# Turns by TensorE transposes, k and v without padding columns, a head start for the second image's front, and x1 added in PSUM in the last image

## The chip, the cores and the metric

The kernel runs on one core of a Trainium2 chip, in one launch. The metric is device time in microseconds (us). Three runs of the kernel before took 5461.75, 5472.33 and 5480.27 us; their median is 5472.33 us. All data are float32.

## What is computed

The input x is a batch of 8 images of 256 channels and 64 x 64 pixels. Two residual layers follow each other; `_gn` is a group norm over groups of 8 channels, without weights:

```python
# layer 0: local attention with 4 heads over 3 x 3 neighbours, and generated kernels
qkv = einsum('oc,bchw->bohw', w_qkv, gn(x))          # q, k, v of 256 channels each
attn = softmax(sum_d(q * k_patch), over 9 neighbours)
kernel = einsum(w_kg, qkv by head) + b_kg            # 4 heads x 9 weights at each pixel
x1 = x + w_proj @ (alpha * sum(kernel * v_patch) + beta * sum(attn * v_patch))
# layer 1: modulated deformable 3 x 3 convolution
om = conv3x3(gn(x1), w_off) + b_off                  # 27 = 18 offsets + 9 mask values
v = bilinear_samples(gn(x1), 9 taps, offsets) * sigmoid(mask)
out = x1 + einsum('bckhw,ock->bohw', v, w)
```

## The kernel before, in words

An image is cut into 8 chunks of 8 rows (512 pixels); 256 channels lie as 2 tiles of 128 partitions. There are two streams of work.

The **front** of an image is a Python generator (`fronts`) that issues 144 steps. The first 126 are `attention`. After four steps of group norm (means, an empty one, the standard deviation with `ready`, the first `normed`), each chunk takes 14 steps: the spread weights of the chunk before, q, k(0), k(1), products(0), products(1), logits, generated, v(0), turned, v(1), project, weights, keys. The work on a chunk's output is finished during the steps of the next chunk. The last 18 steps are `prepare`: per chunk, one step turns the 27 offset values of the chunk before to pixel-major (`positions`) and writes normed pixels to a table in DRAM (`to_table`), and one step runs the 3 x 3 offset convolution (`offsets`).

The **slots** of an image are 72, one for each chunk and tap (8 x 9). A slot gathers 4 blocks of 128 rows from the table by indirect DMA (`gather`, L820, on POOL), scales the first corner (`scale`, L836, on ACT), adds the three other corners (`sum_corners`, L844, on DVE), transposes the sums on TensorE (`transposes`, L865, with copies by ACT at L868), and multiplies them with the convolution weights into the PSUM tile `po` (`product`, L890). After 9 taps `finished` copies `po` to `y` (ACT, L901) and `stored` adds x1 (DVE, L906) and sends the chunk out (SP).

The order on every engine is the order of the Python program (`manual_schedule`); each engine runs its own instructions strictly in that order, and waits are semaphores between engines. The main loop at the end of the kernel runs over 577 slots in two halves each. In each half it issues the slot's work, and then as many front steps of the next image as the `goal` (L963) asks for: one for each half slot, and 12 more spread over the first image (`STEPS_AHEAD`). So the whole front of image 0 runs alone, then 7 images of slots run with the front of the next image between them, and the slots of the last image run alone. The gathers run 18 blocks ahead of the transposes.

Places that matter for what follows:

- `keyed` (L329 to 343), called by `k` and `v`: a step computes 4 rows for both channel tiles, 264 columns for each matmul since the 2 padding columns of each row are computed too, and ACT copies PSUM to `kt` (L349) or, in overlapping 10-column tiles, to `vt` (L358).
- `generated` and `turned` (L405 to 439): the 36 generated kernel values come out of TensorE in two halves of 64 partitions, one for each channel tile; ACT copies them (L417). Four float32 matmuls with `gs` as weights and the constant `stk_gen` as moving operand turn them and add the two halves in one (L427); DVE adds the bias (L435).
- `offsets` and `positions` (L695 to 775): the same for the 27 offset values, which come out in four groups of 32 partitions; four matmuls with `stk_om` turn and add them (L718), ACT makes the mask (L732), DVE computes positions from PSUM (L735) and then indices and weights (L736 to L768). DVE's L735 waits for ACT's L732, since both read one PSUM tile.
- A chunk's `r` is a tile for x1 of images 0 to 6, loaded from DRAM by SP (L877).
- `psum_a` hands out four PSUM buffers in turn, for nearly all front work.

Of the kernel before, what the change touches and what calls it, by code (L numbers as in the profile page):

```python
# [9 lines left out]
F32 = mybir.dt.float32  # L10
I32 = mybir.dt.int32
AF = mybir.ActivationFunctionType
# [5 lines left out]
P = 128  # L18
C = 256
# [32 lines left out]
LEAD = SCALE_AHEAD + GATHERS  # L52
STEPS = 2 * SLOTS
STEPS_AHEAD = 12


@with_exitstack
def preact_kernel(ctx: ExitStack, tc: tile.TileContext, a: dict, out: bass.AP):
# [34 lines left out]
    def const_tile(name, shape, queue=nc.scalar):  # L93
        t = const.tile(shape, F32, tag=name, name=name)
        queue.dma_start(t, a[name])
        return t
# [12 lines left out]
        load_chunk(0, c, nc.scalar)  # L109
    alpha = const_tile("alpha", [P, 1])  # L110
    gmat = const_tile("gmat", [P, P])
    bkg = const_tile("bkg", [P, HEADS * KK])
    w_qkvT = const_tile("w_qkvT", [P, NT, 3 * C])
    ident = const_tile("ident", [P, P])
    near_k = const_tile("near_k", [P, NK])
# [8 lines left out]
    stk_om = const_tile("stk_om", [P, NOM], nc.sync)  # L124
    stk_gen = const_tile("stk_gen", [P, HEADS * KK], nc.sync)
# [15 lines left out]

    kt = const.tile([P, NT, R + 2, WP], F32, tag="k", name="k")
    vt = const.tile([P, NT, TC, KT, KT], F32, tag="v", name="v")

    w_effT = const.tile([P, NT, P // 2], F32, tag="w_effT", name="w_effT")
    nc.vector.memset(w_effT, 0.0)
# [25 lines left out]
    def psum_a(name):  # L172
        return ps_a.tile([P, 512], F32, tag="a", name=name)
# [86 lines left out]
            )  # L260
        return xn

    def tiled(ps, rows):

        t = ps[:, : rows * WP].rearrange("p (r w) -> p r w", w=WP)
        t = t[:, :, 0 : TC * T].rearrange("p r (t x) -> p t r x", x=T)
        ap = [list(d) for d in t.ap]
        ap[-1][1] = KT
        return bass.AP(tensor=t.tensor, offset=t.offset, ap=ap)

    def window(t, ct, k):
        dy, dx = divmod(k, 3)
# [17 lines left out]
    class Attention:  # L290
# [35 lines left out]
                    vt[:, :, :, R : R + 2, :].rearrange("p c t y x -> p (c t) (y x)"),  # L326
                )

        def keyed(self, which, i, to):  # L329

            for lo, hi in [(0, 2)] * (self.c == 0 and i == 0) + [(2 + 4 * i, 6 + 4 * i)]:
                for m in range(NT):
                    ps = psum_a(f"ps{'qkv'[which]}_{self.u}_{lo}_{m}")
                    o = which * C + m * P
                    for ct in range(NT):
                        nc.tensor.matmul(  # L336
                            ps[:, : (hi - lo) * WP],
                            w_qkvT[:, ct, o : o + P],
                            self.xn[:, ct, lo:hi, :],
                            start=(ct == 0),  # L340
                            stop=(ct == NT - 1),
                        )
                    to(m, lo, hi, ps)

        def k(self, i):
            self.keyed(
                1,
                i,
                lambda m, lo, hi, ps: nc.scalar.copy(  # L349
                    kt[:, m, lo:hi, :].rearrange("p r w -> p (r w)"), ps[:, : (hi - lo) * WP]  # L350
                ),
            )

        def v(self, i):
            self.keyed(
                2,
                i,
                lambda m, lo, hi, ps: nc.scalar.copy(vt[:, m, :, lo:hi, :], tiled(ps, hi - lo)),  # L358
            )

        def products(self, jj):

# [42 lines left out]
        def generated(self):  # L405

            ps = psum_a(f"gen_{self.u}")
            for ct in range(NT):
                nc.tensor.matmul(
                    ps[64 * ct : 64 * ct + 64, :],  # L410
                    w_effT[:, ct],
                    window(self.xn, ct, 4),
                    start=True,
                    stop=True,
                )
            self.gs = gs = p1.tile([P, N], F32, tag="gs", name=f"gs_{self.u}")
            nc.scalar.copy(  # L417
                gs.rearrange("p (t y x) -> p y t x", y=T, x=T),
                ps.rearrange("p (y t x) -> p y t x", y=T, x=T),
            )  # L420

        def turned(self):

            ps = psum_a(f"gt_{self.u}")
            n = HEADS * KK
            for j in range(NB):
                nc.tensor.matmul(  # L427
                    ps[:, j * n : (j + 1) * n],
                    self.gs[:, j * P : (j + 1) * P],
                    stk_gen,  # L430
                    start=True,
                    stop=True,
                )
            self.kb = kb = p1.tile([P, self.G, KK], F32, tag="kb", name=f"kb_{self.u}")
            nc.vector.tensor_add(  # L435
                kb.rearrange("p (j h) k -> p j (h k)", j=NB),
                ps[:, : NB * n].rearrange("p (j k) -> p j k", j=NB),
                bkg.unsqueeze(1).to_broadcast([P, NB, n]),
            )

        def softmax_1(self):
# [228 lines left out]
    def prepare(b, gn):  # L670
# [43 lines left out]
        def positions(c, om):  # L714
            u = f"{b}_{c}"
            ps = psum_a(f"omt_{u}")
            for j in range(NB):
                nc.tensor.matmul(  # L718
                    ps[:, j * NOM : (j + 1) * NOM],
                    om[:, j * P : (j + 1) * P],  # L720
                    stk_om,
                    start=True,
                    stop=True,
                )
            omt = ps[:, : NB * NOM].rearrange("p (b o) -> p b o", o=NOM)
            S = [P, NB, 2 * KK]

            def small(name, shape=S, dt=F32):
                return p1.tile(shape, dt, tag=name, name=f"{name}_{u}")

            mk = small("mk", [P, NB, KK])
            nc.scalar.activation(mk, omt[:, :, 18:27], AF.Sigmoid)  # L732

# [137 lines left out]
    def product(b, n, m):  # L871

        c, k = divmod(n, KK)
        if k == KK // 2 and m == 0:
            r = p1.tile([P, NT, N], F32, tag="r", name=f"r_{b}_{c}")
            if b + 1 < B:
                nc.sync.dma_start(r, kept[b % 2][:, :, c * N : (c + 1) * N])  # L877
            state["r"] = r
        if k == 0 and m == 0:

            if b + 1 == B and c % 2:
                state["po"] = [psum_a(f"po_{b}_{c}_{i}") for i in range(NT)]
            else:
                po = ps_o.tile([P, NT, 512], F32, tag="o", name=f"po_{b}_{c}")
                state["po"] = [po[:, i, :] for i in range(NT)]
        po, v = state["po"], state["v", n]
        if m == NT - 1:
            del state["v", n]
        for ct in range(NT):
            nc.tensor.matmul(  # L890
                po[m],
                w_conv[:, ct, k, m * P : (m + 1) * P],
                v[:, ct, :],
                start=(k == 0 and ct == 0),
                stop=(k == KK - 1 and ct == NT - 1),
            )

    def finished(b, c, m):
        if m == 0:
# [17 lines left out]
    with tc.manual_schedule(engines=ordered):  # L917
# [2 lines left out]
            first_stats(0, c)  # L920
        fold(ps)
        steps = fronts()
        done = 0
        while done < STEPS:
            next(steps, None)
            done += 1
# [12 lines left out]
        gather(SUM_AHEAD + GATHERS + 1)  # L939
        last = None  # L940
        for n in range(B * SLOTS + 1):
# [3 lines left out]
            for m in range(NT):  # L945
# [14 lines left out]
                        stored(*last, slice(m, m + 1))  # L960

                h = NT * n + m + 1
                goal = h * STEPS + min(h, STEPS) * STEPS_AHEAD  # L963
                while (done - STEPS) * STEPS < goal:
                    next(steps, None)
                    done += 1


def _constants():
# [17 lines left out]
    stk_om = np.zeros((P, NOM), f)  # L987
    for g in range(4):
        stk_om[32 * g : 32 * g + NOM] = np.eye(NOM, dtype=f)
    base = np.zeros((P, NC * NB, KK, 2), f)  # L990
    base[..., 0] = (2 * np.arange(NC * NB)[None, :, None] + p[:, None, None] // W) + k // 3 - 1
    base[..., 1] = (p[:, None, None] % W) + k % 3 - 1
# [4 lines left out]
        "near_k": np.concatenate([near.T, near.T]),  # L997
        "turn_y": turn_y,
        "turn_x": turn_x,
        "stk_om": stk_om,  # L1000
        "stk_gen": np.tile(np.eye(P // 2, HEADS * KK, dtype=f), (2, 1)),
        "base": base.reshape(P, NC * NB, 2 * KK),
        "ident": np.eye(P, dtype=f),
    }
# [2 lines left out]
def _laid_out(x, w_qkv, w_kg, b_kg, alpha, beta, w_proj, w_off, b_off, w):  # L1007
# [2 lines left out]
    off[..., :NOM] = w_off.reshape(NOM, NT, P, KK).transpose(2, 1, 3, 0)  # L1010
    boff = np.zeros((P, 1), np.float32)
    boff[:NOM, 0] = b_off
    return {
        "x": x.reshape(x.shape[0], C, L),
        "w_qkvT": w_qkv.reshape(3 * C, NT, P).transpose(2, 1, 0),
        "w_qkv": w_qkv.reshape(8, 96, C).transpose(1, 0, 2),
        "w_kgT": w_kg.reshape(HEADS, KK, 2, 96).transpose(3, 0, 2, 1).reshape(96, 8, KK),
        "bkg": np.broadcast_to(b_kg.reshape(1, HEADS * KK), (P, HEADS * KK)),
        "alpha": np.broadcast_to(alpha.reshape(1, 1), (P, 1)),
        "beta": np.broadcast_to(beta.reshape(1, 1), (P, 1)),  # L1020
        "w_projT": w_proj.reshape(C, NT, P).transpose(2, 1, 0),
# [24 lines left out]
```

## Time and profile before

One profiled execution took 5417.27 us, with a span of 5415.5 us from its first to its last instruction. It is shorter than the median of the plain runs by 55.06 us (1.0%).

| what | number |
|---|---|
| median of three runs | 5472.33 us |
| profiled execution, its span | 5417.27 us, 5415.5 us |
| mean granted TensorE clock | 0.942 |
| gather DMA issues on POOL (L820) | 2304, 1291 ns mean |
| corner sums on DVE (L844) | 6912, 2811.7 us busy |
| convolution matmuls (L890) | 4608 instructions, 2255.0 us busy |
| k and v matmuls (L336) | 2176 instructions, 254.5 and 259.5 us busy |
| turn of the generated kernels (L427) | 512 instructions, 69.3 us busy |
| turn of the offsets (L718) | 512 instructions, 63.1 us busy |
| adds of x1 in the last image (L906) | 7 of 1214 ns, 2 of 693 ns |

In the profile, PE is TensorE's matmuls, PEld its weight loads, DVE the VectorE, ACT the ScalarE, POOL the GpSimd (which issues the gathers), and SP the queue of the plain DMAs. A float32 matmul that is not a transpose shows as two instructions, each with a weight load (2304 calls at L890 give 4608 instructions); a transpose shows as one. The mean duration of a matmul [...] overlaps with the next one, so for throughput the busy time of a group, or the distance from one start to the next, is read.

### The profile page before, as it was taken

The numbers are of one execution on the slowest core, as the hardware profiler recorded it, in microseconds if no ns is written. First come the engines' busy times: TensorE is split into PE (matmuls) and PEld (weight loads), VectorE is DVE, ScalarE is ACT, GpSimd is POOL, SyncE is SP. The second block draws the span as 40 slices with busy tenths as digits, with TensorE's granted clock in tenths as the row PEclk, the third lists the DMA queues.
The fourth block names the chain that finished last, engine by engine and source line by source line (L and its number), as shares of the span: only waits on it lengthen the run. The fifth ranks groups of instructions, "written<-read, shape, count | busy, mean of one in ns | idle before, by whom it ended". The sixth has DMA issues, their size and how long they took to land. (4 is left out here: it accounts for less than half of the span.)

```text
span 5415.5 us, 80013 instructions
## 1 busy us (share of the span) xinstructions
PE 4849.9 (90%) x26848; PEld 2762.1 (51%) x26848; DVE 4185.3 (77%) x10066; ACT 2447.4 (45%) x5312; POOL 2976.4 (55%) x2310
## 2 busy tenths in 40 slices
PE   8989999999898999999999998989999899987777
PEld 5545554555545555555555555455554555543333
DVE  5577878787787877878788787877878787777666
ACT  3344444444444444444444444444444444444343
POOL 0045554655555556455555555565654655656776
PEclk9999999999999999999999999999999999998888
DMA  2177779777697778877788777877779777688877
GB/s 91 55 253 259 253 244 330 245 249 271 242 330 270 254 264 286 307 249 262 251 310 286 265 256 256 313 266 263 260 244 332 249 248 265 235 288 307 306 268 264
DMA packets 472650, 1414.24 MB, mean 261 GB/s; under 512 B 46815, under 2 KB 114655, under 8 KB 472109
## 3 DMA queue, kind: packets, MB, share of 16 engines
q0 software_dynamic: 331776, 1208.11, 63.4%
q1 hardware_dynamic: 138444, 197.65, 10.3%
q8 instruction: 211, 3.46, 0.2%
q10 hardware_dynamic: 2016, 3.38, 0.2%
q14 instruction: 203, 1.65, 0.1%
HBM read 1276.02 MB, written 132.94 MB: 260 GB/s over the span
## 5 line engine op out<-in xcount | busy, mean ns | idle before, releaser
L820 POOL DMA_INDIRECT g<-table,idx x2304 | 2973.9, 1291 | 2418.0 <-DVE s L844 808.9
L844 DVE SCALAR_TENSOR_TENSOR s<-g,wt,s 128x256 f32<-128x256 f32 x6912 | 2811.7, 476 | 307.6 <-ACT s L836 240.7
L890 PE MATMUL po<-vt,w_conv 128*128 128x512 f32 x4608 | 2255.0, 616 | 33.9 <-ACT y L901 22.4
L836 ACT ACTIVATE s<-g,wt 128x256 f32<-128x256 f32 x2304 | 1068.2, 510 | 574.8 <-DMA g<-table,idx 471.4
L890 PEld LDWEIGHTS po<-vt,w_conv 128*128 128x128 f32 x4608 | 842.0, 198 | 816.8 <-issue 760.1
L868 ACT COPY vt<-pt 128x512 f32<-128x512 f32 x1152 | 618.2, 588 | 528.9 <-PE pt L865 352.5
L865 PE MATMUL pt<-ident,s 128*128 128x128 f32 x4608 | 698.1, 294 | 170.1 <-ACT vt L868 125.6
L865 PEld LDWEIGHTS pt<-ident,s 128*128 128x128 f32 x4608 | 569.3, 151 | 402.6 <-ACT vt L868 166.3
L383 DVE TENSOR_TENSOR qk<-qk,near_k 128x400 f32<-128x400 f32 x256 | 135.4, 567 | 545.8 <-remote 445.7
L375 PE MATMUL qk<-k,q 64*64 64x100 f32 x4096 | 207.4, 268 | 166.5 <-issue 162.1
L304 PE MATMUL psq<-xn,w_qkvT 128*128 128x512 f32 x512 | 258.4, 650 | 65.0 <-DVE wk L516 63.5
L556 ACT COPY acc<-av 128x512 f32<-128x512 f32 x128 | 75.1, 587 | 483.3 <-PE av L549 337.4
L702 PE MATMUL om<-xn,w_off 128*32 128x512 f32 x2304 | 288.6, 596 | 0.6 <-DVE pos L735 0.5
L375 PEld LDWEIGHTS qk<-k,q 64*64 64x64 f32 x4096 | 137.0, 139 | 291.3 <-issue 253.5
L336 PE MATMUL psv<-xn,w_qkvT 128*128 128x264 f32 (+1 forms) x1088 | 259.5, 383 | 0.0
L336 PE MATMUL psk<-xn,w_qkvT 128*128 128x264 f32 (+1 forms) x1088 | 254.5, 379 | 0.0
L336 PEld LDWEIGHTS psv<-xn,w_qkvT 128*128 128x128 f32 x1088 | 201.5, 191 | 85.3 <-issue 49.5
L336 PEld LDWEIGHTS psk<-xn,w_qkvT 128*128 128x128 f32 x1088 | 201.7, 190 | 82.6 <-issue 38.8
L561 PE MATMUL proj<-acc,w_projT 128*128 128x512 f32 x512 | 240.8, 593 | 0.7 <-ACT acc L556 0.7
L549 PEld LDWEIGHTS av<-wk,vk 100*64 100x64 f32 x4096 | 166.0, 163 | 97.9 <-issue 39.9
L549 PE MATMUL av<-wk,vk 100*64 100x64 f32 x4096 | 190.3, 253 | 26.9 <-issue 21.6
L312 ACT COPY q<-psq 128x512 f32<-128x512 f32 x128 | 74.0, 584 | 310.6 <-PE psq L304 310.6
(94 smaller groups left out, 3397.8 us busy)
## 6 DMA issues: line engine op xcount, KB each, us to landing
table<-ts SPq DMA_DIRECT2D x384, 176.0 KB
g<-table,idx POOLq DMA_INDIRECT x2304
out_dram<-r SPq DMA_DIRECT2D x63, 512.0 KB
x<-in_x_dram SPq DMA_DIRECT2D x61, 512.0 KB
x<-x SPq DMA_DIRECT2D x56, 512.0 KB
r<-x SPq DMA_DIRECT2D x56, 512.0 KB
w_conv<-in_w_conv_dram SPq DMA_DIRECT2D x1, 2304.0 KB
x<-in_x_dram ACTq DMA_DIRECT2D x3, 512.0 KB
```

Source lines behind the costliest of these rows:

```text
L304: nc.tensor.matmul(ps, w_qkvT[:, ct, m * P : (m + 1) * P], window(self.xn, ct, 4), start=(ct == 0), stop=(ct == NT - 1),)
L336: nc.tensor.matmul(ps[:, : (hi - lo) * WP], w_qkvT[:, ct, o : o + P], self.xn[:, ct, lo:hi, :], start=(ct == 0), stop=(ct == NT - 1),)
L375: nc.tensor.matmul(both[h][64 * t : 64 * t + 64, n : n + NK], self.qt[r, ct, o * T * T : (o + 1) * T * T], kt[r, ct, :, T * o : T * o + KT ...
L549: nc.tensor.matmul(av[64 * h : 64 * h + 64, g, t * T * T : (t + 1) * T * T], self.vk[:, t, o : o + 64], self.wk[2 * g + h][:, i * n + t * ...
L561: nc.tensor.matmul(ps, w_projT[:, ct, m * P : (m + 1) * P], self.acc[:, ct].rearrange("p (t y x) -> p y t x", y=T, x=T), start=(ct == 0), ...
L702: nc.tensor.matmul(ps[32 * g : 32 * g + 32, :], w_off[:, ct, k, :], window(xn, ct, k), start=(n < 4), stop=(n >= KK * NT - 4),)
L820: nc.gpsimd.indirect_dma_start(out=g, out_offset=None, in_=tables[b % 2], in_offset=bass.IndirectOffsetOnAxis(ap=found[b, c][0][:, j, k : ...
L836: nc.scalar.activation(s, g[:, 0:C], AF.Copy, scale=w[:, 0:1])
L844: nc.vector.scalar_tensor_tensor(s, g[:, q * C : (q + 1) * C], w[:, q : q + 1], s, ALU.mult, ALU.add)
L865: nc.tensor.transpose(pt[ct][:, j, :], s[:, ct * P : (ct + 1) * P], ident)
L868: nc.scalar.copy(v[:, ct, :], pt[ct].rearrange("p b n -> p (b n)"))
L890: nc.tensor.matmul(po[m], w_conv[:, ct, k, m * P : (m + 1) * P], v[:, ct, :], start=(k == 0 and ct == 0), stop=(k == KK - 1 and ct == NT - 1),
```

## The change

1. `turned` and `positions` use four TensorE transposes (with `ident`) in place of four matmuls with a stacking constant. The partial sums (2 halves, 4 groups) now come out beside each other in PSUM, and a DVE reduce adds them. The bias of the generated kernels moves into ACT's copy; the mask's ACT instruction and DVE's position add now read the reduced tile in SBUF. The two stacking constants are gone.
2. `keyed` computes one channel tile and all 8 rows in a step, without the padding columns: 512 columns for each matmul. The borders of `kt` and `vt` are zeroed once by POOL. v's tiles are copied by two ACT instructions (6 inner tiles, 2 outer ones) in place of one.
3. `STEPS_FIRST = 8`: eight steps of image 1's front are issued before the first slot (four before the first gathers' scales, four between the first sums), and the rest of the 12 steps ahead are spread as before.
4. In the last image a float32 matmul of `ident` with x1 adds x1 into `po` at the last tap; `stored` has no DVE add there and sends `y` out itself.

```diff
+STEPS_FIRST = 7 + 1
...
-    bkg = const_tile("bkg", [P, HEADS * KK])
+    bkg = const_tile("bkg", [P, 1])
...
+    nc.gpsimd.memset(kt, 0.0)
+    nc.gpsimd.memset(vt, 0.0)
...
-            for lo, hi in [(0, 2)] * (self.c == 0 and i == 0) + [(2 + 4 * i, 6 + 4 * i)]:
-                for m in range(NT):
+        def keyed(self, which, m, to):
+            for lo, hi in [(0, 2)] * (self.c == 0) + [(2, R + 2)]:
...
-                            self.xn[:, ct, lo:hi, :],
+                        self.xn[:, ct, lo:hi, 1 : W + 1],
...
+            def to(lo, hi, ps):
+                nc.scalar.copy(
+                    vt[:, m, 1 : TC - 1, lo:hi, :], strided(ps, T, TC - 2, T - 1, KT)
+                )
+                nc.scalar.copy(
+                    strided(vt[:, m, 0, lo:hi, :], (TC - 1) * NK - 1, 2, 1, KT - 1),
+                    strided(ps, W - KT + 1, 2, 0, KT - 1),
+                )
...
-            nc.scalar.copy(
+            nc.scalar.activation(
                 gs.rearrange("p (t y x) -> p y t x", y=T, x=T),
                 ps.rearrange("p (y t x) -> p y t x", y=T, x=T),
+                AF.Identity,
+                bias=bkg,
             )
...
-                nc.tensor.matmul(
-                    ps[:, j * n : (j + 1) * n],
-                    self.gs[:, j * P : (j + 1) * P],
-                    stk_gen,
-                    start=True,
-                    stop=True,
+                nc.tensor.transpose(
+                    ps[:, j * P : (j + 1) * P], self.gs[:, j * P : (j + 1) * P], ident
                 )
...
-            nc.vector.tensor_add(
+            nc.vector.tensor_reduce(
                 kb.rearrange("p (j h) k -> p j (h k)", j=NB),
-                ps[:, : NB * n].rearrange("p (j k) -> p j k", j=NB),
-                bkg.unsqueeze(1).to_broadcast([P, NB, n]),
+                ps.rearrange("p (j c k) -> p j k c", j=NB, c=NT)[:, :, 0:n],
+                AX.X,
+                ALU.add,
             )
...
-                nc.tensor.matmul(
-                    ps[:, j * NOM : (j + 1) * NOM],
-                    om[:, j * P : (j + 1) * P],
-                    stk_om,
...
+                nc.tensor.transpose(
+                    ps[:, j * P : (j + 1) * P], om[:, j * P : (j + 1) * P], ident
+                )
...
+            omt = small("omt", [P, NB, NOM])
+            nc.vector.tensor_reduce(
+                omt,
+                ps.rearrange("p (b g o) -> p b o g", b=NB, g=4)[:, :, 0:NOM],
+                AX.X,
+                ALU.add,
+            )
...
-                stop=(k == KK - 1 and ct == NT - 1),
-            )
+                stop=(b + 1 < B and k == KK - 1 and ct == NT - 1),
+            )
+        if b + 1 == B and k == KK - 1:
+            x1 = image[:, m, c * N : (c + 1) * N]
+            nc.tensor.matmul(po[m], ident, x1, start=False, stop=True)
...
-        r, y = state["r"][:, m], state["y"][:, m]
-        x1 = r if b + 1 < B else image[:, m, c * N : (c + 1) * N]
-        nc.vector.tensor_add(r, y, x1)
+        r = state["y"][:, m]
+        if b + 1 < B:
+            r, y = state["r"][:, m], r
+            nc.vector.tensor_add(r, y, r)
...
+        for n in range(STEPS_FIRST - 4):
+            next(steps, None)
         for i in range(GATHERS):
             gather(i)
...
+            for n in range(2 if i == 0 else 1):
+                next(steps, None)
+        done = STEPS + STEPS_FIRST
...
-                goal = h * STEPS + min(h, STEPS) * STEPS_AHEAD
-                while (done - STEPS) * STEPS < goal:
+                goal = h * STEPS + min(h, STEPS) * (STEPS_AHEAD - STEPS_FIRST)
+                while (done - STEPS - STEPS_FIRST) * STEPS < goal:
```

More of the change, by code (lines that the diff above doesn't have):

```diff
@@ L123, in preact_kernel @@
     b_off = const_tile("b_off", [P, 1], nc.sync)
-    stk_om = const_tile("stk_om", [P, NOM], nc.sync)
-    stk_gen = const_tile("stk_gen", [P, HEADS * KK], nc.sync)
     base = const_tile("base", [P, NC * NB, 2 * KK], nc.sync)
@@ L261, in normed, with strided @@
         return xn
-    def tiled(ps, rows):
-        t = ps[:, : rows * WP].rearrange("p (r w) -> p r w", w=WP)
-        t = t[:, :, 0 : TC * T].rearrange("p r (t x) -> p t r x", x=T)
+    def strided(t, step, n, offset, size):
         ap = [list(d) for d in t.ap]
-        ap[-1][1] = KT
-        return bass.AP(tensor=t.tensor, offset=t.offset, ap=ap)
+        return bass.AP(
+            tensor=t.tensor, offset=t.offset + offset, ap=[ap[0], [step, n], *ap[1:-1], [1, size]]
+        )
     def window(t, ct, k):
@@ L327, in carry_v @@
                 )
-        def keyed(self, which, i, to):
-            for lo, hi in [(0, 2)] * (self.c == 0 and i == 0) + [(2 + 4 * i, 6 + 4 * i)]:
-                for m in range(NT):
[L333 to L338, printed above, removed]
-                            self.xn[:, ct, lo:hi, :],
-                            start=(ct == 0),
-                            stop=(ct == NT - 1),
-                        )
-                    to(m, lo, hi, ps)
@@ L345, in k @@
-        def k(self, i):
-            self.keyed(
[L347 to L351, printed above, removed]
-            )
[L354 to L359, printed above, removed]
+        def keyed(self, which, m, to):
+            for lo, hi in [(0, 2)] * (self.c == 0) + [(2, R + 2)]:
+                ps = psum_a(f"ps{'qkv'[which]}_{self.u}_{lo}_{m}")
+                o = which * C + m * P
+                for ct in range(NT):
+                    nc.tensor.matmul(
+                        ps[:, : (hi - lo) * W],
+                        w_qkvT[:, ct, o : o + P],
+                        self.xn[:, ct, lo:hi, 1 : W + 1],
+                        start=(ct == 0),
+                        stop=(ct == NT - 1),
+                    )
+                to(lo, hi, ps[:, : (hi - lo) * W].rearrange("p (r w) -> p r w", w=W))
@@ new lines, in k, with v @@
+        def k(self, m):
+            self.keyed(
+                1, m, lambda lo, hi, ps: nc.scalar.copy(kt[:, m, lo:hi, 1 : W + 1], ps)
+            )
+        def v(self, m):
+            def to(lo, hi, ps):
[6 more added lines that the diff above has]
+                )
+            self.keyed(2, m, to)
@@ L717, in positions @@
             for j in range(NB):
-                nc.tensor.matmul(
-                    ps[:, j * NOM : (j + 1) * NOM],
-                    om[:, j * P : (j + 1) * P],
-                    stk_om,
-                    start=True,
-                    stop=True,
+                nc.tensor.transpose(
+                    ps[:, j * P : (j + 1) * P], om[:, j * P : (j + 1) * P], ident
                 )
-            omt = ps[:, : NB * NOM].rearrange("p (b o) -> p b o", o=NOM)
             S = [P, NB, 2 * KK]
@@ L874, in product @@
         if k == KK // 2 and m == 0:
-            r = p1.tile([P, NT, N], F32, tag="r", name=f"r_{b}_{c}")
             if b + 1 < B:
+                r = p1.tile([P, NT, N], F32, tag="r", name=f"r_{b}_{c}")
                 nc.sync.dma_start(r, kept[b % 2][:, :, c * N : (c + 1) * N])
-            state["r"] = r
+                state["r"] = r
         if k == 0 and m == 0:
@@ L922, in preact_kernel @@
         steps = fronts()
-        done = 0
-        while done < STEPS:
+        for n in range(STEPS):
             next(steps, None)
-            done += 1
+        for n in range(STEPS_FIRST - 4):
+            next(steps, None)
         for i in range(GATHERS):
@@ L986, in _constants @@
     turn_x = turns[p % T % 3]
-    stk_om = np.zeros((P, NOM), f)
-    for g in range(4):
-        stk_om[32 * g : 32 * g + NOM] = np.eye(NOM, dtype=f)
     base = np.zeros((P, NC * NB, KK, 2), f)
@@ L999, in _constants @@
         "turn_x": turn_x,
-        "stk_om": stk_om,
-        "stk_gen": np.tile(np.eye(P // 2, HEADS * KK, dtype=f), (2, 1)),
         "base": base.reshape(P, NC * NB, 2 * KK),
@@ L1012, in _laid_out @@
     boff[:NOM, 0] = b_off
+    bkg = np.zeros((P, 1), np.float32)
+    bkg[: HEADS * KK, 0] = b_kg.reshape(HEADS * KK)
     return {
@@ L1017, in _laid_out @@
         "w_kgT": w_kg.reshape(HEADS, KK, 2, 96).transpose(3, 0, 2, 1).reshape(96, 8, KK),
-        "bkg": np.broadcast_to(b_kg.reshape(1, HEADS * KK), (P, HEADS * KK)),
+        "bkg": bkg,
         "alpha": np.broadcast_to(alpha.reshape(1, 1), (P, 1)),
```

## The prediction, made before the changed kernel ran

> **What bounds the kernel now.** I read the page's first part, then the busy times by stage (stretches of the span), then the timeline of TensorE alone, and last the waits. The page says who is fullest:
>
> ```profile
> PE 4849.9 (90%) x26848; PEld 2762.1 (51%) x26848; DVE 4185.3 (77%) x10066; ACT 2447.4 (45%) x5312; POOL 2976.4 (55%) x2310
> ```
>
> An average over stages proves nothing, so the stages. The columns are start:end, length, busy us of PE, PEld, DVE, ACT, POOL, then clock, DMA share, GB/s. In order: attention of image 0 alone, its prepare alone, the wait for the first gathers, attention of image 2 between slots, its prepare between slots, and what is left when the last front has ended:
>
> ```profile
> 21.00:243.00 222.00, 208.77 (x1748) 136.42 (x1748) 126.25 (x244) 79.00 (x174) 0.00 (x0) 0.98 0.11 41
> 243.00:310.00 67.00, 57.47 (x450) 27.82 (x450) 40.51 (x128) 21.06 (x41) 0.00 (x0) 0.95 0.63 197
> 310.00:335.00 25.00, 7.43 (x27) 5.29 (x27) 17.40 (x52) 8.84 (x18) 18.04 (x19) 0.56 0.85 317
> 943.00:1484.00 541.00, 494.69 (x2724) 291.93 (x2724) 418.49 (x972) 250.35 (x549) 316.44 (x240) 0.95 0.72 249
> 1484.00:1591.00 107.00, 102.30 (x620) 51.91 (x621) 96.43 (x264) 52.51 (x110) 52.31 (x47) 0.98 0.99 368
> 4843.00:5415.00 572.00, 416.35 (x1253) 205.94 (x1251) 387.41 (x940) 227.27 (x478) 397.64 (x298) 0.85 0.76 284
> ```
>
> Attention between slots is TensorE's: 494.69 of 541 us, 91%, with DVE at 77%. Prepare between slots has two full engines: TensorE 96%, DVE 90%. In the last stretch nobody is full; the chain of waits there is made of gathers landing. So time taken from TensorE pays in attention (7 images of about 540 us), pays in prepare (7 of about 107 us) only as far as DVE follows, and pays nothing in the last image.
>
> **Turns and k, v on TensorE.** The timeline of PE alone in image 0's attention, where no slot disturbs, gives prices from start to start:
>
> ```profile
> 149.56 0.63 PE L495 MATMUL w<-ident,wts 128*128 128x128 f32 x4 [0.59 <-DVE wts L483]
> 150.02 1.88 PE L561 MATMUL proj<-acc,w_projT 128*128 128x512 f32 x4
> ...
> 154.59 3.71 PE L304 MATMUL psq<-xn,w_qkvT 128*128 128x512 f32 x8
> 158.14 3.72 PE L336 MATMUL psk<-xn,w_qkvT 128*128 128x264 f32 x16
> 161.79 1.82 PE L375 MATMUL qk<-k,q 64*64 64x100 f32 x64
> ...
> 169.75 1.08 PE L427 MATMUL gt<-stk_gen,gs 128*128 128x36 f32 x8
> 170.67 1.58 PE L336 MATMUL psv<-xn,w_qkvT 128*128 128x264 f32 x6
> ```
>
> Four matmuls that turn the generated kernels take 8 instructions and 170.67 - 169.75 = 0.92 us. Four transposes of 128 columns of the same shape (L495) take 150.02 - 149.56 = 0.46 us. Gain 0.46 us a chunk. Here a rule speaks against the change: the Trainium skill, "TensorE: Matmul & The Clock Gate", section "Back-to-back issue gap", has a matmul cost by its moving columns, with a floor of about 25 ns. By it 8 instructions of 36 columns take 0.2 us, as much as four transposes of 128, and the gain would be nil. The rows say 0.92 against 0.46, so each instruction is paid by its weight load, and half the instructions are half the time. I take the rows. Part 4 of that page adds that transposes don't count as activity for the clock; 0.46 us between other matmuls is too short to matter, and w's transposes lie in a stretch at 0.98.
>
> k takes 3.65 us (161.79 - 158.14) for 16 instructions of 264 columns; unpadded it is 8 of 512, the shape of q, which takes 3.55 us. So k and v gain 0.10 us each: the padding is 3% of the columns, and halving the instructions brings nothing, since these are bound by columns.
>
> Attention thus gives up 0.46 + 0.20 = 0.66 us a chunk, 56 x 0.66 = 37 us in the seven overlapped images. How much arrives? The longest entry among PE's waits in image 2's attention (us in total, times, longest):
>
> ```profile
> PE qk L375 <- issue: 23.4, 35, 1.7
> ```
>
> The next is 9.1 us for the spread weights' DVE products (L516). Neither is fed by what is removed, and neither hangs on an engine that gets much more to do: DVE's load rises by 0.14 us a chunk there (below), ACT's falls. What could take its place is an ACT scale waiting for a gather with k's copies behind it. I count nine tenths, -33 us; bounds -18 and -37.
>
> ACT: k's copies go from 4 x 377 to 2 x 584 ns (q's copy has that shape), v's from 4 x 430 ns to two pairs, estimated from the rows at 264 to 512 columns as 560 + 280 ns: -0.34 and -0.04 us a chunk. The bias in the copy costs 687 - 585 = 0.10 us (L711 against L417). With ACT at 46% this is free. Fewer PSUM buffers are taken in turn (4 less a chunk), free as well. POOL's two more memsets, about 1.2 us each like its others at the start, lie before the first normed pixels at 21 us.
>
> **DVE's reduces.** A reduce of 432 inputs, and the add that is replaced:
>
> ```profile
> L480 DVE TENSOR_REDUCE kb<-tx 128x144 f32<-128x432 f32 x64 | 38.6, 603 | 2.2
> L435 DVE TENSOR_TENSOR kb<-gt,bkg 128x144 f32<-128x144 f32 x64 | 19.6, 306 | 159.3 <-PE pt L865 51.4 <-PE gt L427 48.5 <-remote 48.2
> ```
>
> A reduce of 144 inputs (L445) takes 295 ns, so it is 1.07 ns an input: 288 inputs (kernels) 0.45 us, +0.14 us on the add; 432 inputs (offsets) 0.60 us, all new, since the position add stays.
>
> **Prepare between slots** is where this decides. Two chunks of image 4, DVE alone, then PE alone:
>
> ```profile
> 2816.92 0.22 DVE L735 TENSOR_TENSOR pos<-omt,base 128x72 f32<-128x72 f32 x1
> ...
> 2827.42 0.22 DVE L735 TENSOR_TENSOR pos<-omt,base 128x72 f32<-128x72 f32 x1
> ```
>
> ```profile
> 2816.38 1.04 PE L865 MATMUL pt<-ident,s 128*128 128x128 f32 x8
> ...
> 2825.30 0.97 PE L718 MATMUL omt<-stk_om,om 128*128 128x27 f32 x8
> 2826.11 1.49 PE L682 MATMUL ptab<-ident,xn 128*88 128x128 f32 x12
> 2827.44 0.82 PE L865 MATMUL pt<-ident,s 128*128 128x128 f32 x6
> ```
>
> No line shows a bracket, so neither engine idles: DVE's own cycle is 10.50 us (it lags and catches up), TensorE's is 11.06 us. The turn takes 0.81 us here and will take 0.46: TensorE 10.71. DVE gets 0.60: 11.10. The bound changes hands, from 11.06 to 11.10, +2 us over 56 chunks; I take +3. The bounds are -20 us (56 x 0.35, if DVE's reduce fills what are now its waits for ACT's mask, "DVE pos <- ACT mk", 63 us in all, which go: the add reads SBUF) and +34 us (56 x 0.60). The new waits: DVE's reduce waits for the transposes with the sums behind it, as L735 did; ACT's mask now waits for DVE, with three table copies and the slot's copies behind it, which wait up to DVE's lag (0.3 to 2.8 us in the trace) and have half of ACT's time as cover.
>
> **Image 0 alone.** In attention the last wait is the bracket 0.59 before the weights' transposes: the turn is 0.46 earlier, the reduce 0.14 later, k and half of v 0.15 earlier, so 0.47 x 8 = -3.8 us. In prepare, DVE has 1.8 us of idle before each L735, which covers the reduce, and TensorE's 0.35 is saved: -3 us. Together -7.
>
> **Eight steps first.** They are the norm's two small matmuls, ACT's table load (1.28 us) and square root, the normed chunk (two DVE instructions, 1.65 us), q and k of chunk 0 (about 8 us of TensorE with the two extra rows) and six copies. No DMA is among them, so SP and POOL are passed by nothing. TensorE idles from 310 to 335 us but for 7.43 us and at a clock of 0.56; the first gather lands some 4 us after its issue, and DVE's sums follow landings. The normed pixels end some 8 us after the first gather's issue, when the second gather has just landed, so the sums lose about 1 us and TensorE fills its hole: -8 us, bounds 0 (the early slots wait for gathers) and -14 (a warm clock too, the first eight `po` took 5.63 us where warm ones take 3.5).
>
> **Last image.** 16 matmuls more are 32 instructions of 0.43 us, 14 us, beside 572 - 416 = 156 us of idle TensorE; DVE's 9.9 us less are hidden too. At the very end four instructions (1.7 us) stand where a DVE add (0.69 us) stood: +1 us. Bounds 0 and +14 (cover gone).
>
> **Sum.** -33 - 7 - 8 + 3 + 1 = -44 us against the profiled 5417.27: 5373. The runs' median is 1.0102 of the profiled time; 5373 x 1.0102 = 5428 us.
>
> **Rivals.** (A, slower) DVE sets prepare and drags the others in a ring: reduce, ACT's mask, table copies, slot copies, TensorE. A chunk then grows by 0.60 + 0.20 + 1.55 (three table copies) - 0.35 = 2.0 us, 56 of them +112 us; with the other terms +65, so 5538. For it: DVE back to back at 10.50. Against: the copies behind the mask feed the next slot's products, most of a cycle later. It makes the kernel slower from 1.1 us a chunk. 13%.
> (B, no change) Attention's saving is half eaten by gathers that hold ACT (in image 2 TensorE waited 1.33 us behind such a scale), prepare gets 0.3 us longer, the start gives nothing: -16 - 7 + 17 + 1 = -5, so 5467. 13%.
> (C, larger) All of 37, prepare -20, start -14, image 0 -7, end +1: -77, so 5395. 14%.
> The forecast itself, 5410 to 5450: 60%.
>
> A measurement here can tell about 0.3% (16 us) from no change. Faster: forecast, C and a piece of B, 75%; same 12%; slower 13%. The range 5390 to 5475 takes in C nearly and B, and leaves out A.
>
> **What would show it.** Right: gt and omt with 256 instructions each and some 0.46 us for four; k and v at 512 columns without change of busy time; attention windows 4 to 5 us shorter an image; prepare windows within 3 us of 107 with DVE at 95%; a clock near 1 and q, k in the hole after 310 us; the last stretch the same length. Wrong: reduces far over 0.6 us, ACT's mask waiting long for DVE, or prepare over 115 us.

## The result, and the profile after

The changed kernel takes 5434.89 us, the median of 20 runs (5417.74 to 5463.96); the kernel before, run beside it, takes 5467.0 us (20 runs, 5455.74 to 5499.17). The ratio is 0.9935, with a 95% interval of 0.9921 to 0.9949: faster by 0.65%, some 35 us. The forecast was 5428 us.

The two traces cannot show this by their spans. The profiled execution of the changed kernel took 5421.1 us (span 5419.2 us); that of before, 5417.27 us, lies below all 20 of its plain runs. So the stages are read, not the spans. Of the page after, the engine totals and the groups of k and v:

```profile
PE 4819.7 (89%) x25344; PEld 2523.2 (47%) x25344; DVE 4217.9 (78%) x10121; ACT 2434.2 (45%) x5200; POOL 2971.2 (55%) x2312
...
L337 PE MATMUL psv<-xn,w_qkvT 128*128 128x512 f32 (+1 forms) x576 | 248.9, 558 | 1.3 <-DVE kb L438 1.3
L337 PE MATMUL psk<-xn,w_qkvT 128*128 128x512 f32 (+1 forms) x576 | 246.3, 557 | 0.0
```

TensorE has 1504 instructions less; k and v cost 8.2 and 10.6 us less than before (254.5 and 259.5). The stretches of the changed kernel, in the order and the columns in which the prediction showed those of before:

```profile
21.00:241.00 220.00, 203.45 (x1588) 108.04 (x1587) 127.03 (x242) 78.93 (x160) 0.00 (x0) 0.98 0.11 40
241.00:305.50 64.50, 54.81 (x420) 24.63 (x420) 44.85 (x136) 20.48 (x41) 0.00 (x0) 0.95 0.64 206
305.50:335.00 29.50, 13.83 (x85) 8.28 (x88) 17.58 (x50) 9.44 (x21) 18.14 (x18) 0.72 0.85 321
943.80:1478.00 534.20, 490.10 (x2565) 261.96 (x2565) 422.33 (x980) 249.59 (x535) 316.18 (x241) 0.95 0.74 255
1478.00:1586.00 108.00, 100.48 (x589) 47.98 (x589) 98.51 (x268) 50.96 (x108) 51.60 (x46) 0.98 0.97 361
4836.00:5419.00 583.00, 429.90 (x1286) 214.18 (x1284) 378.02 (x932) 226.20 (x479) 401.73 (x298) 0.85 0.74 279
```

Image 0 alone is shorter in both stages (222.00 to 220.00, 67.00 to 64.50). The hole before the first slot holds twice the TensorE work (7.43 to 13.83) at a better clock (0.56 to 0.72). Image 2's attention is 7 us shorter, but this is one image: over images 2 to 7 the mean goes from 537.4 to 536.4 us, and single images lie up to 10 us apart, so these two traces do not carry the 4 to 5 us an image that were forecast. Image 2's prepare is as long as before (107.00, 108.00), with TensorE down from 96 to 93% and DVE at 91%. The last row is longer, 583 against 572; it is 587 us in `nox1` too, the kernel below that does without part 4.

The prices, in the timeline of PE in image 0's attention:

```profile
153.46 3.60 PE L337 MATMUL psk<-xn,w_qkvT 128*128 128x512 f32 x8
156.99 0.58 PE L380 MATMUL qk<-k,q 64*64 64x100 f32 x16
...
165.10 0.65 PE L434 MATMUL gt<-ident,gs 128*128 128x128 f32 x4
165.59 1.88 PE L337 MATMUL psv<-xn,w_qkvT 128*128 128x512 f32 x4
```

k takes 156.99 - 153.46 = 3.53 us (forecast 3.55), the turn 0.49 us (forecast 0.46, before 0.92). The rule that was set aside, a matmul priced by its moving columns, would have left the turn as it was. The section of the Trainium skill that the prediction names ("TensorE: Matmul & The Clock Gate", "Back-to-back issue gap") states this rule for a matmul on its own, without its weight load, and says that in a stream of weight loads and matmuls both set the spacing. The traces agree with that part of it: the turn's weight loads stand back to back, 8 in 0.97 us before (169.75) and 4 in 0.42 us after (165.09). The granted clock of image 0's two stages, with more transposes in them, stays at 0.98 and 0.95. And the two reduces (line, shape, count, then busy us and mean ns):

```profile
L438 DVE TENSOR_REDUCE kb<-gt 128x144 f32<-128x288 f32 x64 | 29.2, 456 | 152.0 <-remote 70.8 <-PE pt L872 45.3 <-PE gt L434 24.8
...
L732 DVE TENSOR_REDUCE omt<-omt 128x108 f32<-128x432 f32 x64 | 38.5, 601 | 35.5 <-PE omt L722 33.4 <-issue 2.1
```

0.456 and 0.601 us, against 0.45 and 0.60 worked out from other reduces.

### The profile page after: what moved, and what is told of

It is laid out like the page before. It is cut to its first block, busy times and chain, and to the rows that moved or that the text cites. A ratio compares the mean times of both kernels' runs of the same rounds, so it can differ in the third digit from the quotient of the medians.

```text
span 5419.2 us, 76847 instructions
## 1 busy us (share of the span) xinstructions
PE 4819.7 (89%) x25344; PEld 2523.2 (47%) x25344; DVE 4217.9 (78%) x10121; ACT 2434.2 (45%) x5200; POOL 2971.2 (55%) x2312
## 5 line engine op out<-in xcount | busy, mean ns | idle before, releaser
L380 PEld LDWEIGHTS qk<-k,q 64*64 64x64 f32 x4096 | 141.0, 140 | 315.2 <-issue 268.5
L337 PE MATMUL psv<-xn,w_qkvT 128*128 128x512 f32 (+1 forms) x576 | 248.9, 558 | 1.3 <-DVE kb L438 1.3
L337 PE MATMUL psk<-xn,w_qkvT 128*128 128x512 f32 (+1 forms) x576 | 246.3, 557 | 0.0
L306 PEld LDWEIGHTS psq<-xn,w_qkvT 128*128 128x128 f32 x512 | 102.1, 208 | 234.8 <-DVE wk L520 129.4
L540 ACT COPY vk<-vk 100x512 f32<-100x512 f32 x256 | 137.3, 587 | 149.2 <-PE vk L535 143.9
```

The costliest lines, as they stand in the source:

```text
L306: nc.tensor.matmul(ps, w_qkvT[:, ct, m * P : (m + 1) * P], window(self.xn, ct, 4), start=(ct == 0), stop=(ct == NT - 1),)
L337: nc.tensor.matmul(ps[:, : (hi - lo) * W], w_qkvT[:, ct, o : o + P], self.xn[:, ct, lo:hi, 1 : W + 1], start=(ct == 0), stop=(ct == NT - 1),)
L380: nc.tensor.matmul(both[h][64 * t : 64 * t + 64, n : n + NK], self.qt[r, ct, o * T * T : (o + 1) * T * T], kt[r, ct, :, T * o : T * o + KT ...
```

## The experiments

The theory under test (T1 where an expectation names it) is the prediction's: TensorE sets attention, so its saved time arrives there; DVE takes over prepare at about the old length; the last image covers what TensorE is given. Each expectation names what the other reading of its part would give. The first eight kernels ran on one chip ("the first chip" below; the kernel before takes 5459 and 5467 us there, as it did in the runs of the result), the last four on another, each time with the kernel before beside them. Brackets hold 95% intervals of the ratio to the kernel before; a difference in us is worked out from the ratio unless the medians are named.

### Each part alone

Each kernel is the kernel before with one numbered part of the change, by the lines of the diff above (shortened and joined here).

`turns`, part 1:

```diff
-                nc.tensor.matmul(ps[:, j * n : (j + 1) * n], self.gs[:, j * P : (j + 1) * P], stk_gen, ...)
+                nc.tensor.transpose(ps[:, j * P : (j + 1) * P], self.gs[:, j * P : (j + 1) * P], ident)
...
+            nc.vector.tensor_reduce(omt, ps.rearrange("p (b g o) -> p b o g", b=NB, g=4)[:, :, 0:NOM], AX.X, ALU.add)
```

> The kernel before with the turns alone (transposes and DVE reduces in both places, bias in ACT's copy). Theory T1, TensorE's time in attention: 56 x 0.46 us x 0.9 = -23, image 0 alone -6, prepare +3, so -26 us. Theory T2, the gain follows the number of TensorE instructions (1024 rows of weight loads and matmuls go here, 2048 with k and v): about -10 us. Theory T3, the gain lies in image 0 alone and nothing arrives between slots: -6 us.

Measured: 5445.11 us (12 runs) beside 5459.23; ratio 0.9963 [0.9943, 0.9983], -20 us (-31 to -9); the medians differ by 14. T3's -6 is out; T1's -26 and T2's -10 both lie inside.

`kv`, part 2:

```diff
-                            ps[:, : (hi - lo) * WP],
+                        ps[:, : (hi - lo) * W],
```

> The kernel before with k and v unpadded alone. T1: 56 x 0.20 us x 0.9 and image 0's 1.2 us, so -11 us. T2 (instructions count): -20 us or more, twice the turns. T3: -1 us.

Measured: 5450.02 us; 0.9979 [0.9959, 0.9999], -11 us (-22 to -1), which T1 and T2 both fit. One part saves TensorE 0.46 us a chunk in attention, the other 0.20, and -20 and -11 stand in about that proportion, but the intervals are too wide to show it. What speaks against T2 is the timeline above: k with half the instructions takes 3.53 us in place of 3.65.

`steps`, part 3:

```diff
+        for n in range(STEPS_FIRST - 4):
+            next(steps, None)
         for i in range(GATHERS):
             gather(i)
```

> The kernel before with eight steps ahead of the first slot alone. T1: -8 us (0 to -14), k of two half chunks among them. T2: 0. If ACT's stall of 8 us that the changed kernel's trace shows at 324.5 to 333.0 us comes with these steps and takes their gain: 0, and slot 20 starts no earlier than before.

Measured: 5463.87 us; 1.0003 [0.9984, 1.0022], +2 us (-9 to +12). By itself the head start shows no gain on this chip, though the interval just takes in the forecast -8.

`x1`, part 4:

```diff
+        if b + 1 == B and k == KK - 1:
+            nc.tensor.matmul(po[m], ident, x1, start=False, stop=True)
...
-        nc.vector.tensor_add(r, y, x1)
```

> The kernel before with x1 added in PSUM in the last image alone. T1: +1 us (0 to +2), the 14 us of TensorE lie beside idle time; if the cover were gone: +14. T2: 0.

Measured: 5479.81 us; 1.0036 [1.0015, 1.0058], +20 us. Part 4 costs time, and by more than its 14 us of TensorE instructions would if nothing hid them, though the interval (+8 to +32) does not exclude 14. It excludes the forecast +1.

### The whole change, less a part or with a cost doubled

`nox1`, the changed kernel without part 4:

```diff
-            nc.tensor.matmul(po[m], ident, x1, start=False, stop=True)
...
+        nc.vector.tensor_add(r, y, x1)
```

> The changed kernel without its fourth part: x1 is added by DVE in the last image as before. T1 (each part as predicted): 1 us under the changed kernel, a ratio of 0.993 to the kernel before. If the 0.36% that the fourth part alone cost is its own and adds up: some 20 us under the changed kernel, a ratio of 0.990. Theory L, single parts move the time by some 0.3% either way through where the instructions come to lie: no fixed expectation, anything from 0.990 to 0.997.

Measured: 5423.99 us (6 runs) beside 5466.53; 0.9912 [0.9889, 0.9934], -43 us. This version beats both kernels by the medians; against the whole change it is 0.0023 better, some 12 us, with intervals that overlap: the difference is known to about 14 us.

`noom`, the changed kernel with the offsets' turn of before:

```diff
-                nc.tensor.transpose(ps[:, j * P : (j + 1) * P], om[:, j * P : (j + 1) * P], ident)
+                nc.tensor.matmul(ps[:, j * NOM : (j + 1) * NOM], om[:, j * P : (j + 1) * P], stk_om, ...)
...
-            nc.vector.tensor_reduce(omt, ...)
```

> The changed kernel, but the offsets' turn is the one before (four stacking matmuls, no DVE reduce, the mask read from PSUM). T1, prepare has two full engines and the exchange of 0.35 us of TensorE for 0.60 us of DVE is worth nothing there: the changed kernel's time (image 0's prepare gives back 3 us, prepare between slots gains 3). If TensorE sets prepare: +20 us, 0.997. If DVE sets it and ACT's mask wait hurts: -20 us or more, 0.990.

Measured: 5431.05 us; 0.9931 [0.9908, 0.9954], the same as the whole change to about 15 us. The offsets' transposes and their reduce cancel to that accuracy; 0.997 and 0.990 are out.

`red2`, the changed kernel with the offsets' reduce done twice:

```diff
             nc.vector.tensor_reduce(omt, ...)
+            nc.vector.tensor_reduce(omt, ...)
```

> The changed kernel with the offsets' DVE reduce done twice (0.60 us of DVE for each chunk, 0.6 x 64 = 38 us more of DVE). T1, DVE sets prepare now: +0.6 x 56 = +34 us and some of image 0's, so back to the time before, 0.999 to 1.000. If TensorE still sets prepare: 0 to +5 us, 0.994.

Measured: 5466.17 us; 1.0003 [0.9982, 1.0023]. 56 further reduces of 0.60 us between slots are 34 us; the time rose by 0.0068 x 5467 = 37 us by the ratios, by 31 by the medians. Nothing hides DVE's time in prepare now: in the trace the last five of the seven cycles from chunk to chunk in image 2's prepare take TensorE 11.0 to 12.4 us. In image 7's, where DVE has no next image's statistics to make, all seven take 10.67 us, the second reduce included.

`pe4`, the changed kernel with the four transposes of the generated kernels done twice:

```diff
-            for j in range(NB):
+            for j in [*range(NB), *range(NB)]:
```

> The changed kernel with the generated kernels' four transposes done twice (0.46 us of TensorE for each chunk, no other engine has more to do). T1, TensorE sets attention: +0.46 x 56 x 0.9 = +23 us and +3 in image 0, 0.998 to 0.999. Theory T3 (TensorE's time between slots is covered): +3 us, 0.994.

Measured: 5453.39 us; 0.9966 [0.9949, 0.9982], +17 us by the ratios and +18.5 by the medians. 64 x 0.46 = 29 us of TensorE were added, so some six tenths of TensorE's time in attention show in the end; the forecast had counted nine tenths of its saving. The 17 us are known to about 12: T3's +3 is out, nine tenths are not.

### On another chip

There the kernel before takes 4833.36 us (17 runs, 4821.73 to 4850.68), at a granted clock of 0.984 in place of 0.942. The same instructions with almost the same durations take 12% less, and TensorE is nearly always busy between slots. Its attention stages vary by 3 us from image to image in place of 10, so they carry what the first chip's could not.

`before2`, the kernel before, for a second profile:

> The kernel before once more, for a second profile: the first one's execution (5417 us) lies below all of its plain runs. If its stages are typical, attention between slots is again about 533 us and prepare 108 us an image; if that execution was a lucky one, attention is 537 to 540 us, and the changed kernel's gain of 4 to 5 us an image shows.

Measured: 4840.42 us, span 4838.6. It does not answer the question as put, since it is another chip's trace. But the attention of image 2 between slots is 470 us there, not 541:

```profile
888.90:1359.30 470.40, 462.00 (x2724) 271.89 (x2724) 418.65 (x974) 250.84 (x550) 320.77 (x240) 0.99 0.81 287
1359.30:1465.80 106.50, 101.92 (x617) 52.30 (x618) 95.55 (x262) 52.14 (x108) 49.22 (x46) 0.98 0.98 368
```

TensorE is 98% busy in attention (462.00 of 470.40) and 96% in prepare: the bound is the one that the prediction named, and purer.

`turnskv`, parts 1 and 2 of the change alone:

```diff
+                nc.tensor.transpose(ps[:, j * P : (j + 1) * P], om[:, j * P : (j + 1) * P], ident)
...
+                        ps[:, : (hi - lo) * W],
```

> The kernel before with the first two parts alone (turns by transposes, k and v unpadded), no steps ahead of the first slot, no x1 in PSUM. By the parts measured one at a time (-20 and -11 us): -31 us, ratio 0.994. If the head start is worth the prediction's 8 us once the turns are short, the changed kernel without part 4 is 8 us faster than this one; if it is worth nothing, the two are the same, 0.991 to 0.992.

Measured: 4809.73 us (6 runs); 0.995 [0.993, 0.997], -24 us. The two parts alone multiply to 0.9942 on the first chip; within the intervals they add.

`yadd`, the changed kernel without part 4's matmul, but with the sum made in `y` and sent from there:

```diff
+        if b + 1 == B:
+            r = y
         nc.vector.tensor_add(r, y, x1)
```

> The changed kernel without its last part, but in the last image DVE adds x1 into y in place, and y is sent (as part 4 sends it), not r: so the tile that ACT copies the next chunk's sums into is free only when the DMA out has read it. TensorE gets nothing to do. If part 4's price is this wait for the DMA out: +11 us beside the changed kernel without part 4, ratio 0.993. If it is TensorE's time: 0 us, ratio 0.991.

Measured: 4802.74 us (6 runs); 0.9928 [0.9906, 0.9951], -31 us. The interval takes in both 0.993 and 0.991, so the traces have to tell. From the end of the last front to the end of the span it takes 463.30 us, `turnskv`, which sends `r`, 465.30. So on this chip sending `y` costs nothing that shows.

`pe56`, the changed kernel without part 4, with matmuls in the last image whose result nobody reads:

```diff
+        if b + 1 == B and k == KK - 1:
+            ps = psum_a(f"more_{c}_{m}")
+            for i in range(4):
+                nc.tensor.matmul(ps, ident, x1, start=(i == 0), stop=(i == 3))
```

> The changed kernel without its last part (DVE adds x1), and in the last image, at the last tap of each chunk and channel tile, four float32 matmuls of ident with x1 into a PSUM tile that nobody reads: 64 matmuls, 128 instructions of 0.43 us, 55 us of TensorE; the output is the reference's. If TensorE's time in the last image is covered by its idle time (156 us before the change), as the prediction had it: 0 to +2 us beside the changed kernel without part 4 (5424), ratio 0.991. If that cover is gone, which would explain what x1 on TensorE cost (11 to 20 us for a quarter of these instructions): +25 to +55 us, ratio 0.996 to 1.001.

Measured: 4820.01 us (12 runs); 0.9964 [0.9952, 0.9977], 17 us above `yadd` (0.0036 x 4833). The last image of `yadd`, then of `pe56`:

```profile
4334.70:4798.00 463.30, 395.76 (x1256) 188.19 (x1254) 389.20 (x941) 231.71 (x479) 348.70 (x298) 0.95 0.90 351
```

```profile
4336.40:4821.90 485.50, 431.47 (x1384) 212.77 (x1382) 388.85 (x941) 229.15 (x479) 364.41 (x298) 0.95 0.87 335
```

128 instructions of 0.43 us, 55 us, lengthen it by 22.2 us in the traces and by 17 in the runs: 30 to 40% is not covered, though TensorE idles for 67 us there in `yadd`. (`pe56` sends `r` and `yadd` sends `y`, which is the difference that `yadd` itself found to cost nothing.) The waits show how (us in all, times, longest), of ACT and DVE in the last image, `yadd` first:

```profile
ACT y L908 <- PE po L897: 12.4, 7, 4.1
ACT vt L875 <- PE pt L872: 7.0, 4, 3.1
DVE s L851 <- ACT s L843: 53.9, 43, 4.9
```

```profile
ACT vt L875 <- PE pt L872: 40.9, 21, 3.2
ACT y L913 <- PE po L897: 22.4, 10, 4.6
DVE s L851 <- ACT s L843: 75.5, 55, 4.9
```

While TensorE does the extra work, the next slot's transposes come late, and ACT, in its order, stands at their copies (7.0 to 40.9 us) and at the chunk's copy, with the scales of later slots behind it; DVE's waits for those scales grow from 53.9 to 75.5 us. At the very end nothing is beside it: the last slot, from its transposes to the end, takes 16.8 us against 13.3, which is 8 x 0.43.

## Why the prediction was right, and where not

**Sum.** It said -44 us and 5428; the runs gave -32 by the medians, -35 by the ratio. Without part 4 it would have said -45, and `nox1` gave -43. That agreement is closer than the terms deserve, and in part luck: `nox1` is known to about 12 us, and on the second chip the same parts gave -31 by the runs. The terms that follow, -25, +2, -9 and -7 on that chip, add to -39; the traces of `before2` and `yadd` lie 41 us apart. Rival A (a ring through DVE, 5538) and B (no change, 5467) are out, and C (5395) needed gains in prepare that did not come.

**Attention between slots, -33.** The mechanism was right, the size too high. On the second chip, where the stages are steady, attention of images 2 to 7 takes 471.15 us on average in the kernel before and 467.6 in `turnskv`, `yadd` and `pe56` (467.63, 467.47, 467.60): 3.55 us an image, -25 in seven, against 37 of saved TensorE time: 0.68 of it. `pe4` gave 0.6 on the first chip by the runs. Nine tenths should have been two thirds. The step that failed is the list of waits: the prediction took TensorE's wait for DVE's products of the spread weights as one that the change would leave alone. It grows. All such waits of TensorE, in `before2` and then in `yadd`:

```profile
PE psq L304 <- DVE wk L516: 7.4, 20, 0.9
PE av L549 <- DVE wk L516: 2.0, 8, 0.3
```

```profile
PE psq L306 <- DVE wk L520: 13.3, 23, 1.3
PE av L553 <- DVE wk L520: 3.8, 15, 0.4
```

From 9.4 to 17.1 us in all, this is 8 of the 12 us that did not arrive. The likely reason is that TensorE, with less work of its own, comes to q and to the weighted sums before DVE is done; no run changed DVE's work there.

**Prepare between slots, +3.** The bound changed hands as forecast. Two chunks of image 4 in the changed kernel, DVE, then PE:

```profile
2817.74 0.60 DVE L732 TENSOR_REDUCE omt<-omt 128x108 f32<-128x432 f32 x1
...
2829.06 0.60 DVE L732 TENSOR_REDUCE omt<-omt 128x108 f32<-128x432 f32 x1
```

```profile
2816.27 0.60 PE L722 MATMUL omt<-ident,om 128*128 128x128 f32 x4
...
2826.94 0.60 PE L722 MATMUL omt<-ident,om 128*128 128x128 f32 x4
```

DVE's cycle is 11.32 us without a bracket (forecast 11.10), TensorE's 10.67 (10.71). DVE thus falls behind by 0.65 us a chunk, and the prediction did not say where that is paid. It is paid in two places. The first is the end of the same stage: once DVE's reduce starts some 2.8 us after the transposes' end, TensorE waits for the normed pixels that it turns for the table, and goes at DVE's pace. Three chunks later in the same prepare, PE:

```profile
2859.67 0.60 PE L722 MATMUL omt<-ident,om 128*128 128x128 f32 x4
...
2860.83 1.40 PE L686 MATMUL ptab<-ident,xn 128*88 128x128 f32 x11 [0.41 <-issue]
...
2870.99 0.60 PE L722 MATMUL omt<-ident,om 128*128 128x128 f32 x4
2872.30 1.77 PE L686 MATMUL ptab<-ident,xn 128*88 128x128 f32 x12 [0.71 <-DVE xn L256]
...
2882.84 0.60 PE L722 MATMUL omt<-ident,om 128*128 128x128 f32 x4
```

Here the cycles are 11.32 and 11.85 us, so the first chunks' gain (10.67 against 11.06 before) is lost again by the last ones. The second place is the next image's norm, for which TensorE waits. Before, then after, the end of image 2's prepare:

```profile
1589.76 0.97 PE L718 MATMUL omt<-stk_om,om 128*128 128x27 f32 x8
...
1595.90 0.38 PE L187 MATMUL gn<-mv,gmat 128*128 128x2 f32 x2 [2.53 <-DVE mv L182]
```

```profile
1585.13 0.60 PE L722 MATMUL omt<-ident,om 128*128 128x128 f32 x4
...
1592.22 0.59 PE L190 MATMUL gn<-mv,gmat 128*128 128x2 f32 x2 [3.90 <-DVE mv L185]
```

The stretch from the end of the last `omt` to `gn`, averaged over the six borders between images, is 5.1 to 5.2 us in every kernel with the old offsets' turn (`noom` too), 6.5 in every one with the new and 7.6 in `red2`, alike on both chips: 6 x 1.3 = +8 us. Prepare itself is even in images 2 to 6 (105.4 to 105.2 us on average on the second chip). In image 7 DVE has no next image's statistics to make, all seven cycles of TensorE are 10.67 us, and it goes from 105.5 to between 100.7 and 103.4. Over all seven images the mean goes from 105.8 to 104.9, -6 us in all. Together with the borders that is +2 where +3 stood, and within the intervals it equals the old turn in time (`noom`). The size was met, but by a longer border and a shorter last prepare that the prediction did not have: that is luck.

**Image 0 alone, -7.** Its prepare takes 67.4 to 68.3 us in kernels with the old turn of the offsets and 63.4 to 65.5 in those with the new: -3, as forecast. Its front ended at 310.4 us before and at 305.6 and 306.8 in the changed kernel and `nox1` (-4.8, -3.6); on the second chip at 315.2 and, in `yadd` and `turnskv`, 306.5 and 302.5 (-8.7, -12.7), which do the same work up to there. The clock of the attention stage varies there (0.96, then 0.98 and 0.99), so the rest of the term is good to a few us only.

**Eight steps first, -8.** Seen on the second chip, not on the first. From the end of image 0's front to slot 72 `yadd` takes 601.3 us and `turnskv` 607.9: -6.6. The runs of the two differ by 7 us as well, with intervals that overlap. The hole before the first slot, of the kernel before and of `yadd`:

```profile
315.20:340.00 24.80, 6.96 (x24) 4.96 (x24) 18.08 (x53) 9.37 (x19) 17.96 (x19) 0.56 0.86 318
```

```profile
306.50:330.00 23.50, 15.51 (x112) 9.49 (x112) 19.67 (x55) 10.56 (x23) 15.94 (x17) 0.78 0.81 298
```

TensorE works in it as forecast. But the early slots lose more than the 1 us that was allowed: the first transposes come 19.0 us after the front's end, not 11.5, and slot 8 is 8 us late. The gain comes at the other end of the image, where eight steps are no longer to be done. On the first chip the same sum is about -2.5 (mean of six kernels with the steps, 682.4, and four without, 684.9), and `steps` alone +2 with an interval of -9 to +12; the ten sums spread from 675.5 to 689.8, so -2.5 is no finding. There, in the changed kernel, the first products stood behind k's copies, which ACT could not begin although the matmuls had ended by 324.7 us:

```profile
333.68 1.61 PE L380 MATMUL qk<-k,q 64*64 64x100 f32 x32 [7.58 <-ACT k L348]
```

Part of the head start probably went into delays of that kind, which the last section tells of; that was not tried.

**Last image, +1.** This step failed: "beside 572 - 416 = 156 us of idle TensorE" took an average as a cover. The +1 at the very end is there (the last slot takes 1.0 us more with part 4), but part 4 costs 20 us alone (+8 to +32) and some 12 under the whole change, where 0 is not excluded. `pe56` shows that of time given to TensorE at a chunk's end a third is not covered, for the reason shown above. For part 4 that makes 14 x 0.35 = 5 us, an estimate from the second chip; the bound of +14 for a lost cover was the better guess. What stays open is the rest. 5 lies below the interval of `x1`; `yadd` speaks against the sending of `y`, but on the other chip; part 4 itself was not run there, so it is not known whether the first chip makes it dearer. The first chip's traces do not place it: from the end of the last front to the end of the span `x1` takes 575.5 us and the kernel before 572.9, the changed kernel 583.5 and `nox1` 586.8, and the ten kernels on that chip spread from 569 to 599. Theory L, that the time moves with where the instructions lie, was not tested. A version with the generated kernels' transposes, k, v and the steps, but without part 4 and without the offsets' turn, was not tried; by `noom` it should equal `nox1` to about 15 us.

## What to carry to other kernels

Idle time of an engine covers new work only where the work can wait: at the end of a chunk of the last image the next transposes queue behind it, and a third of it showed though the engine was idle for a seventh of the stage. When an edit moves the bound of a stage from one engine to another and both are even, ask where the lag of the new one is collected; here it was the last chunks of the stage and the next stage's first result. When work is taken from an engine, expect its other waits to grow into the gap: here a fifth of the saving went there. Read small changes from stages that repeat, in several kernels, since one profile's span can lie 1% off the median.

## What the runs showed of the hardware that was not expected

The kernel before takes 5467 us on one chip and 4833 on another, and the two traces name a difference. The group of DVE's first product on the first chip, then on the second:

```profile
L383 DVE TENSOR_TENSOR qk<-qk,near_k 128x400 f32<-128x400 f32 x256 | 135.4, 567 | 545.8 <-remote 445.7
```

```profile
L383 DVE TENSOR_TENSOR qk<-qk,near_k 128x400 f32<-128x400 f32 x256 | 133.6, 566 | 192.2 <-PE qk L375 173.7
```

The instruction is the same to a nanosecond; on the first chip DVE idles 354 us more before it, released by "remote", that is by no end of work that the profile can match. In that trace TensorE's completed matmuls are not reported to the other engines for up to 17 us at a time: counted as stretches of over 1.5 us in which a matmul with a semaphore update had ended and no update of TensorE's appears, there are about 235 of them with about 1.05 ms in the kernel before, 216 with 1.00 ms in the changed one, and 200 to 240 in every kernel on that chip. On the second chip there are 2 with 5.6 us in the kernel before, 1 in `turnskv` and none in `yadd` and `pe56`. Traffic alone does not explain them: in image 2's attention the second chip moves more than the first (287 against 249 GB/s in the rows of the kernel before). But they do come with heavy traffic: over the first chip's late stretches in the kernel before the DMA moves 355 GB/s on average, against 261 over the whole execution. What makes the updates late was only seen, not tried, and how much of the 634 us between the chips it explains stays open; the clock of attention differs too (0.95 and 0.99). The gain in per cent is the same on both within the intervals (`nox1` 0.9912, `yadd` 0.9928).
